# Left-over rows of a quadratic form: six passes from five operand tiles, and a 32-row by 64-column tiling for the rest

## The chip, the cores and the metric

The kernel runs on one core of one Trainium2 chip. The metric is the device time of one execution in microseconds (us); lower is better. The core has a matrix engine (TensorE, PE in the profile), a vector engine (VectorE, DVE), a scalar engine (ScalarE, ACT), GpSimd (POOL), and a queue engine for transfers (SyncE, SP). Each runs its own instruction stream; semaphores order them. SBUF is the on-chip memory of 128 partitions; PSUM, with eight banks of 512 float32 columns per partition, takes the results of TensorE.

## The reference

The input x has 1024 samples, 39 fields and 64 embedding columns. Three layers are computed; each is bilinear in the layer before and in x:

```python
def _cin_layer(Xk, X0, W, b):
    Wr = W.reshape(O, Hk, Fdim)
    return jnp.einsum('bhe,bfe,ohf->boe', Xk, X0, Wr) + b[None, :, None]
X0 = sparse_embedding; Xk = X0
for W, b in ((W0, b0), (W1, b1), (W2, b2)):
    Xk = _cin_layer(Xk, X0, W, b)
    outs.append(Xk.sum(axis=-1))
return jnp.concatenate(outs, axis=-1) @ fc_w.T + fc_b
```

All layers have 64 outputs. Only sums over the embedding columns, weighted by fc_w, leave the function, so the second and third layer can be folded. Call A the 64 outputs of the first layer before its bias: each is a weighted sum of the 780 products x_a x_b with a <= b. The rest of the answer is a sum over columns and over 64 rows of (A + b0) times Z, where each row of Z is again a weighted sum of the same 780 products, plus a weighted sum of the 39 fields themselves (the linear rows), plus a constant. Small terms from the biases b1 and b2 are added at the end.

## The kernel before, in words

**Blocks.** A column is one sample and one embedding index; there are 65,536. They are worked in 32 blocks of 2048 columns (`BLK`), two blocks to a pair, 16 pairs. One block fills four PSUM banks of 512 columns (`po[n][0..3]`); rows 0 to 63 of a bank hold A, rows 64 to 127 hold Z.

**Operand tiles.** The input is transposed by transfers to DRAM tables `xd` (field by column, with a row of ones after the 39 fields; three tables, each of two blocks). From a table, GpSimd gathers rows into operand tiles of 128 partitions by lists of row numbers (`gather_rows`, L124): four tiles of 128 x 2048 per block (`rt[n % 2][:, 0..3]`, filled by `roll`, L129), and two more per pair, `ut` and `vt`, whose 128 rows are 64 left-over rows of the first block and 64 of the second (`roll_half`, L134). The multiplication of two tiles by VectorE (`product`, L158) gives 128 rows of products; the lists are chosen so that the six pairs of the four tiles give 768 different products and linear rows, and the u-v product the 51 that are left of 819. `prods` has four buffers.

**Passes.** A chunk is one such product with its 128 x 128 weights `wa[:, c]` (64 columns for A, 64 for Z). `multiply` (L478) runs it over the four banks of the block. The chunk of left-over rows is run for both blocks: for each bank two matmuls of 64 rows and 128 columns, on rows 0 to 63 for block n and 64 to 127 for block n+1 (L485 to L493). Every float32 matmul appears in the trace as two matmul records and two weight loads.

**End of a block.** `finish` (L503): ScalarE reads Z of a bank with its constant into `z`, VectorE forms (A + b0) Z into `g`, and a reduction over the 64 embedding indices writes `sums`. `fields` (L495) copies the 39 fields of a block from `ut` into the lower rows of `g`, so that they are summed too.

**Order.** The program order is written out by hand (`manual_schedule`): `steps` lists the chunks, seven for an even block (the left-over chunk last) and six for an odd one. At each step (L583) PE gets the chunk, then possibly `finish` and `fields` of a block that closed a step ago, then VectorE the product four steps ahead (`AHEAD`), and after a block's last product GpSimd the gathers for the block two further on (L606 to L611). The inputs of later blocks are loaded by SP or GpSimd (`load`).

**Preparation.** L169 to L424 load and fold the weights into `both`; GpSimd and VectorE work out the row numbers (`lists`, L261 to L279 and L310 to L319); the first three operand tiles of block 0 are gathered in halves from `xh`, a first copy of the input. `weight_rows` (L427) forms 128 rows of weights of a chunk as runs along diagonals of `both` (one VectorE addition per run, or a ScalarE copy), and `weight_turn` (L463) transposes them on PE and copies them to `wa`. During the first pair this is interleaved with the steps.

Of the kernel before, what the change touches and what calls it, by code (L numbers as in the profile page):

```python
# [61 lines left out]
FH = F * H  # L62
NG = 3
K = NG * F
STEP = (0, 15, 9, 6)
BASE = (0, 3, 5, 20)
LAST = 11
EXTRA = (None, 6, 17, 28)
NX = 11
HR = 64  # L70
PAIRS = ((0, 1), (0, 2), (0, 3), (1, 2), (2, 3), (1, 3))
NPAIR = len(PAIRS)
ORDER = (0, 1, 3, 2, 4, 5)
NCHUNK = NPAIR + 1
# [9 lines left out]
FT = F + 1  # L84
NTAB = 3

_dist = sorted(
    min(d % F, -d % F)
    for i, k in PAIRS
    for j in range(NG)  # L90
    for d in [(STEP[k] - STEP[i]) * j + BASE[k] - BASE[i]]
)
assert sorted(_dist + [LAST]) == list(range(1, F // 2 + 1))
assert max(2 * s + b for s, b in zip(STEP, BASE)) < F
assert K + NX == 128 and EXTRA[1:] == tuple(6 + LAST * i for i in range(3))


@with_exitstack
def cin_kernel(ctx: ExitStack, tc: tile.TileContext, x, w0t, b0, w1, b1, w2, b2, fc_w, fc_b, out):
# [12 lines left out]
    xh = [dram.tile([FT, SUB], F32, name=f"xh{k}") for k in range(2)]  # L112
# [16 lines left out]
    def roll(n):  # L129
        for i in range(4):  # L130
            k = n % 2 * 4 + i
            gather_rows(rt[n % 2][:, i], xd[n // 2 % NTAB][: FT if k < 4 else 2 * FT], k)

    def roll_half(n):  # L134
        for k, dst in enumerate((ut, vt)):
            gather_rows(dst[n // 2 % 2], xd[n // 2 % NTAB], 8 + k)

    wa = const.tile([128, NCHUNK, 2 * H], F32, name="wa")
# [4 lines left out]
    b0s = const.tile([H, 1], F32, name="b0s")  # L143
# [5 lines left out]
    lists = const.tile([128, 10], I32, name="lists")  # L149
    rt = [const.tile([128, 4, BLK], F32, name=f"r{k}") for k in range(2)]  # L150
    ut = [const.tile([128, BLK], F32, name=f"u{k}") for k in range(2)]
    vt = [const.tile([128, BLK], F32, name=f"v{k}") for k in range(2)]
# [5 lines left out]
    def product(n, c, cols=slice(0, BLK), p=None):  # L158
        if p is None:
            p = prods.tile([128, BLK], F32, name="p", tag="p")  # L160
        if c < NPAIR:
            i, k = PAIRS[c]
            r = rt[n % 2]
            nc.vector.tensor_tensor(p[:, cols], r[:, i, cols], r[:, k, cols], ALU.mult)  # L164
        else:
            nc.vector.tensor_tensor(p, ut[n // 2 % 2], vt[n // 2 % 2], ALU.mult)  # L166
        return p

    prep = tc.tile_pool(name="prep", bufs=1)  # L169
    with prep as prep:  # L170
# [11 lines left out]
        shifts = prep.tile([128, 3, 3], F32, name="shifts")  # L182
# [13 lines left out]
        def load_half(k):  # L196
            nc.scalar.dma_start(
                xh[k][0:F].rearrange("f (b e) -> b f e", e=E), x[k * SB : (k + 1) * SB]
            )
# [12 lines left out]
        for i in range(3):  # L212
            for k, by in enumerate((STEP[i + 1], BASE[i + 1], EXTRA[i + 1] - K)):
                nc.gpsimd.memset(shifts[:, k, i : i + 1], float(by))
        for k in range(2):
            nc.gpsimd.dma_start(xh[k][F:FT].rearrange("r (p c) -> p r c", c=128), ones[0:8, 0:1])
# [26 lines left out]
        wide = prep.tile([128, 5, 3], F32, name="wide")  # L243
        fields_of = prep.tile([128, 6], F32, name="fields_of")
        third = prep.tile([128, 1], I32, name="third")
# [15 lines left out]
        row, f0, j, extra, t, half, q = new(), new(), new(), new(), new(), new(), new()  # L261
        field = [fields_of[:, i : i + 1] for i in range(6)]
        nc.vector.tensor_scalar(third, place, 171, None, ALU.mult)
        nc.vector.tensor_copy(row, place)
        nc.vector.tensor_scalar(parity[:, 1:2], place, 1, None, ALU.bitwise_and)
        nc.vector.tensor_scalar(third, third, 9, None, ALU.logical_shift_right)
        step(row, K, 1.0, extra)
        nc.vector.tensor_copy(f0, third)
        nc.vector.tensor_scalar(wide[:, 3], shifts[:, 2], row, None, ALU.add)
        fused(j, f0, -float(NG), row, ALU.mult, ALU.add)  # L270
        nc.vector.tensor_scalar(wide[:, 0], shifts[:, 1], f0, None, ALU.add)
        nc.vector.tensor_scalar(field[0], f0, float(F), None, ALU.min)
        fused(wide[:, 1], shifts[:, 0], j, wide[:, 0], ALU.mult, ALU.add)
        step(wide[:, 1], F, -float(F), wide[:, 2])
        nc.vector.tensor_tensor(wide[:, 1], wide[:, 1], wide[:, 2], ALU.add)
        nc.vector.tensor_tensor(wide[:, 4], wide[:, 3], wide[:, 1], ALU.subtract)
        fused(fields_of[:, 1:4], wide[:, 4], extra, wide[:, 1], ALU.mult, ALU.add)
        nc.vector.tensor_copy(lists[:, 0:4], fields_of[:, 0:4])
        nc.vector.tensor_scalar(lists[:, 4:8], fields_of[:, 0:4], float(FT), None, ALU.add)  # L279
# [5 lines left out]

        nc.gpsimd.memset(pairs, 0.0)
# [22 lines left out]

        step(row, HR, 1.0, half)  # L310
        fused(q, half, -float(HR), row, ALU.mult, ALU.add)
        nc.vector.tensor_tensor(field[4], q, step(q, F, -float(F)), ALU.add)
        nc.vector.tensor_tensor(field[4], field[4], step(q, 56, 11.0), ALU.add)
        nc.vector.tensor_scalar(field[5], q, float(F), None, ALU.min)
        fused(t, q, -50.0, step(q, 45, 1.0), ALU.add, ALU.mult)
        for y in (t, step(q, 50, -float(F)), step(q, 56, -6.0)):
            nc.vector.tensor_tensor(field[5], field[5], y, ALU.add)
        nc.vector.tensor_scalar(half, half, float(FT), None, ALU.mult)
        nc.vector.tensor_scalar(lists[:, 8:10], fields_of[:, 4:6], half, None, ALU.add)  # L319
# [7 lines left out]
        for k, cols in enumerate(halves):  # L327
            nc.sync.dma_start(xd[0][0:F, cols], xh[k][0:F])
        gather_rows(rt[0][:, 3], xd[0][:FT], 3)
# [38 lines left out]
        roll_half(0)  # L368
# [3 lines left out]
        nc.gpsimd.dma_start(b0s, b0.rearrange("(h o) -> h o", o=1))  # L372
# [54 lines left out]
    def weight_rows(c):  # L427
        def put(at, by, n, a, b, sa, sb, twice=True):
            out = pairs[:, c, at : at + by * (n - 1) + 1 : by]
# [5 lines left out]
            if twice:  # L435
                nc.vector.tensor_tensor(  # L436
                    out, diagonal(a, b, sa, sb), diagonal(b, a, sb, sa), ALU.add
                )
            else:
                nc.scalar.copy(out, diagonal(a, b, sa, sb))  # L440

        if c == NPAIR:
            put(0, 1, F, 0, 0, 1, 1, False)
            put(39, 1, 6, 0, F, 1, 0, False)
            put(45, 1, 5, 6, 34, 1, 1)
            put(50, 1, 6, 11, 0, 1, 1)
            put(56, 1, 6, 28, 0, 1, 1)
            nc.vector.tensor_copy(pairs[:, c, HR:], pairs[:, c, 0:HR])
            return
        i, k = PAIRS[c]  # L450
        if i == 0:
            put(K, 1, NX, EXTRA[k], F, 1, 0, False)
        elif k - i == 1:
            put(K, 1, NX, EXTRA[i], EXTRA[k], 1, 1)
        for j in range(NG):
            a, b = STEP[i] * j + BASE[i], STEP[k] * j + BASE[k]
            cuts = sorted({0, F - a, F - b, F})
            for lo, hi in zip(cuts, cuts[1:]):
                put(NG * lo + j, NG, hi - lo, (a + lo) % F, (b + lo) % F, 1, 1)

    turned = []

    def weight_turn(c):  # L463
# [6 lines left out]
        at = slice(place, place + 128)  # L470
        nc.tensor.transpose(tr[:, at], pairs[:, c], unit)  # L471
        nc.scalar.copy(wa[:, c], tr[:, at])  # L472
# [4 lines left out]

    def multiply(n, c, p, quarters=range(BLK // MM)):  # L478
        half = c == NPAIR
        for k in (n, n + 1) if half else (n,):  # L480
            if k not in po:
                po[k] = [bank("po") for _ in range(BLK // MM)]
        for m in quarters:

            for h in range(2 if half else 1):  # L485
                w = slice(h * HR, (h + 1) * HR) if half else slice(0, 128)
                nc.tensor.matmul(  # L487
                    po[n + h][m],
                    wa[w, c, :],
                    p[w, bass.ts(m, MM)],  # L490
                    start=c == opens[n + h],
                    stop=c == closes[n + h],
                )  # L493

    def fields(n):  # L495
        g[n] = []
        h = n % 2 * HR
        for m in range(BLK // SUB):
            gt = work.tile([H + F, SUB], F32, name="g", tag="g")
            nc.scalar.copy(gt[H : H + F], ut[n // 2 % 2][h : h + F, bass.ts(m, SUB)])  # L500
            g[n].append(gt)

    def finish(n):  # L503
        z = [work.tile([H, SUB], F32, name="z", tag="z") for _ in range(BLK // SUB)]
        for m in range(BLK // MM):
            nc.scalar.activation(  # L506
                z[m // 2][:, bass.ts(m % 2, MM)], po[n][m][H:128], AF.Identity, bias=fc0s[H:128]
            )
        for m in range(BLK // MM):
            at = bass.ts(m % 2, MM)  # L510
            gt = g[n][m // 2]
            nc.vector.scalar_tensor_tensor(  # L512
                gt[0:H, at], po[n][m][0:H], b0s, z[m // 2][:, at], ALU.add, ALU.mult
            )
            if m % 2:
                b_at = n * BB + m // 2 * SB
                nc.vector.tensor_reduce(  # L517
                    sums[:, b_at : b_at + SB], gt.rearrange("p (b e) -> p b e", e=E), AX.X, ALU.add
                )

    def finish_quarter(n, m):
        t = work.tile([H, MM], F32, name="zq", tag="zq")
        at = bass.ts(m % 2, MM)
        gt = g[n][m // 2][:, at]
        nc.scalar.activation(t, po[n][m][H:128], AF.Identity, bias=fc0s[H:128])  # L525
# [147 lines left out]
```

## Time and profile before

Three runs: 747.16, 748.48 and 750.84 us, median 748.48. One profiled execution:

| | |
|---|---|
| time of the profiled execution, first to last instruction (its span) | 749.0 us |
| first matmul on an operand tile (line 487) | at 20.6 us |
| last start of such a matmul | at 743.4 us |
| TensorE clock granted | 1.000 |
| matmul records of line 487 | 1792 (112 a pair) |
| one pair of blocks, middle of the run | 45.03 us |
| VectorE busy in such a pair | 39.2 us |
| GpSimd busy in such a pair | 19.1 us |
| DMA, mean over the span | 241 GB/s, 180.40 MB |
| gather of an operand tile, issue to landing | 5.0 / 7.8 / 13.2 us (least, median, most) |

The profile gives no other time for this execution than its span, so sums are made against 749.0 us. In a group of the profile, the number after x is the count of instructions; then the duration of one, or the busy time and the mean of one. "Idle before" is the time an engine stood still just before an instruction, and what ended it. PEld is the weight load of TensorE, which runs beside the matmuls. Matmul ends are modelled, so distances between starts are the better measure of TensorE's pace.

### The profile page before, as it was taken

Reading aid. Unit: us, or ns where it says so; the run is one execution under the profiler, and the core shown is the slowest. Engines: PE = TensorE matmul, PEld = TensorE weight load, DVE = VectorE, ACT = ScalarE, POOL = GpSimd, SP = SyncE. Lnnn points to the kernel's source line nnn. Section 1 sums busy time; section 2 is a strip of 40 time slices with the busy share of each in tenths; the row PEclk is TensorE's granted clock in tenths of the full one; section 3 lists DMA queues with packets and bytes.
Section 4 is the critical chain, followed back from the end, with each engine's and each line's share of the span. In section 5 each row is a group of like instructions: output and inputs, shape, how many; then the busy total and the mean of one; then the engine's idle time right before and its main releaser. Section 6 shows DMA issues by size and latency. Waiting matters only on the chain.

```text
span 749.0 us, 5258 instructions
## 1 busy us (share of the span) xinstructions
PE 744.8 (99%) x1895; PEld 328.9 (44%) x1895; DVE 644.6 (86%) x513; ACT 164.6 (22%) x226; POOL 320.2 (43%) x198
## 2 busy tenths in 40 slices
PE   9999999999999999999999999999999999999998
PEld 6444444444444444444444444444444444444443
DVE  5998898888889888898888889888899888898885
ACT  3132211221212222112221212222112221212222
POOL 7965633336243253633436243263532436343100
PEclk9999999999999999999999999999999999999999
DMA  9989675875757776575876757776565855747400
GB/s 303 380 280 410 212 287 183 336 258 200 292 163 277 258 288 246 183 280 193 336 240 212 280 178 281 259 275 249 182 287 197 336 224 187 271 141 300 168 1 0
DMA packets 58930, 180.40 MB, mean 241 GB/s; under 512 B 37172, under 2 KB 37237, under 8 KB 38808
## 3 DMA queue, kind: packets, MB, share of 16 engines
q0 software_dynamic: 24320, 169.44, 59.4%
q1 hardware_dynamic: 32894, 8.63, 5.0%
q10 hardware_dynamic: 1690, 1.99, 1.0%
q8 instruction: 15, 0.25, 0.1%
q14 instruction: 11, 0.09, 0.0%
HBM read 179.98 MB, written 10.60 MB: 254 GB/s over the span
## 4 chain that ended last, share of the span: by engine, by line
PE 99%; DVE 0%; ACT 0%; issue 0%
PE po L487 96%; PE idle L230 1%; PE pt L389 0%; PE pv L338 0%; PE pv L389 0%; PE pw L349 0%; PE pw L409 0%; PE tr L471 0%; PE pt L409 0%; PE small L296 0%; DVE g L526 0%; DVE sums L528 0%; ACT zq L525 0%; PE small L298 0%; DVE fc L301 0%
## 5 line engine op out<-in xcount | busy, mean ns | idle before, releaser
L487 PE MATMUL po<-p,wa 128*128 128x512 f32 (+1 forms) x1792 | 723.1, 595 | 0.0
L164 DVE TENSOR_TENSOR p<-r 128x2048 f32<-128x2048 f32 (+2 forms) x197 | 434.9, 2236 | 86.2 <-PE po L487 86.2
L487 PEld LDWEIGHTS po<-p,wa 128*128 128x128 f32 (+1 forms) x1792 | 314.0, 190 | 405.3 <-issue 383.7
L125 POOL DMA_INDIRECT r<-xd,lists x125 | 258.1, 2065 | 363.7 <-DVE p L164 336.6
L506 ACT ACTIVATE z<-po,fc0s 64x512 f32<-64x512 f32 x124 | 84.6, 683 | 356.5 <-PE po L487 349.7
L500 ACT COPY g<-u 39x1024 f32<-39x1024 f32 x64 | 66.7, 1043 | 180.2 <-DVE sums L517 180.1
L512 DVE SCALAR_TENSOR_TENSOR g<-po,b0s,z 64x512 f32<-64x512 f32 x124 | 86.4, 734 | 0.0
L517 DVE TENSOR_REDUCE sums<-g 103x16 f32<-103x1024 f32 x62 | 75.6, 1220 | 2.2
L166 DVE TENSOR_TENSOR p<-u,v 128x2048 f32<-128x2048 f32 x16 | 36.5, 2284 | 0.0
L125 POOL DMA_INDIRECT u<-xd,lists x16 | 28.3, 1772 | 4.9 <-issue 4.3
L125 POOL DMA_INDIRECT v<-xd,lists x16 | 15.3, 955 | 4.9 <-issue 4.9
L230 PE MATMUL idle<-const-float32-1.0 128*128 128x256 f32 (+1 forms) x16 | 7.3, 609 | 0.8 <-PEq L660 0.8
L526 DVE SCALAR_TENSOR_TENSOR g<-po,b0s,zq 64x512 f32<-64x512 f32 x4 | 3.0, 743 | 5.3 <-ACT zq L525 5.3
L125 POOL DMA_INDIRECT r<-xh,lists x6 | 5.8, 971 | 1.8 <-issue 1.5
L472 ACT COPY wa<-tr 128x128 f32<-128x128 f32 x7 | 1.9, 266 | 19.8 <-PE tr L471 19.8
L436 DVE TENSOR_TENSOR pairs<-both 128x6 f32<-128x6 f32 (+27 forms) x50 | 5.4, 178 | 0.5 <-ACT both L418 0.5
L230 PEld LDWEIGHTS idle<-const-float32-1.0 128*128 128x128 f32 x16 | 4.8, 328 | 1.6 <-issue 0.7
L119 POOL DMA_DIRECT2D xd<-in_x x5 | 5.2, 1063 | 0.0
L525 ACT ACTIVATE zq<-po,fc0s 64x512 f32<-64x512 f32 x4 | 2.7, 683 | 10.2 <-PE po L487 10.2
L528 DVE TENSOR_REDUCE sums<-g 103x8 f32<-103x512 f32 x4 | 2.7, 686 | 0.1
L624 PE MATMUL py<-sums,wfin 103*1 103x512 f32 (+2 forms) x6 | 2.1, 448 | 0.6 <-DVE sums L528 0.6
L389 PE MATMUL pt<-w1s,v 128*128 128x320 f32 x4 | 2.5, 779 | 0.0
(95 smaller groups left out, 54.0 us busy)
## 6 DMA issues: line engine op xcount, KB each, us to landing
xd<-in_x SPq DMA_DIRECT2D x26, 312.0 KB
r<-xd,lists POOLq DMA_INDIRECT x125, 7.8
xd<-in_x POOLq DMA_DIRECT2D x5, 312.0 KB, 6.1
w2s<-in_w ACTq DMA_DIRECT2D x1, 624.0 KB
w1s<-in_w ACTq DMA_DIRECT2D x2, 312.0 KB
xh<-in_x ACTq DMA_DIRECT2D x2, 156.0 KB
xd<-xh SPq DMA_DIRECT2D x2, 156.0 KB
u<-xd,lists POOLq DMA_INDIRECT x16, 8.9
```

What stands on the lines that cost most here:

```text
L119: engine.dma_start(xd[n // 2 % NTAB][first : first + F].rearrange("f (b e) -> f b e", e=E), xv[:, n * BB : (n + 1) * BB, :],)
L125: nc.gpsimd.indirect_dma_start(dst, None, table, bass.IndirectOffsetOnAxis(ap=lists[:, k : k + 1], axis=0))
L164: nc.vector.tensor_tensor(p[:, cols], r[:, i, cols], r[:, k, cols], ALU.mult)
L166: nc.vector.tensor_tensor(p, ut[n // 2 % 2], vt[n // 2 % 2], ALU.mult)
L230: nc.tensor.matmul(idle[:, 0:cols], nc.const_aps.tensor(1.0, (128, 128), F32), nc.const_aps.tensor(1.0, (128, cols), F32), start=True, sto ...
L436: nc.vector.tensor_tensor(out, diagonal(a, b, sa, sb), diagonal(b, a, sb, sa), ALU.add)
L487: nc.tensor.matmul(po[n + h][m], wa[w, c, :], p[w, bass.ts(m, MM)], start=c == opens[n + h], stop=c == closes[n + h],)
L500: nc.scalar.copy(gt[H : H + F], ut[n // 2 % 2][h : h + F, bass.ts(m, SUB)])
L506: nc.scalar.activation(z[m // 2][:, bass.ts(m % 2, MM)], po[n][m][H:128], AF.Identity, bias=fc0s[H:128])
L512: nc.vector.scalar_tensor_tensor(gt[0:H, at], po[n][m][0:H], b0s, z[m // 2][:, at], ALU.add, ALU.mult)
L517: nc.vector.tensor_reduce(sums[:, b_at : b_at + SB], gt.rearrange("p (b e) -> p b e", e=E), AX.X, ALU.add)
L526: nc.vector.scalar_tensor_tensor(gt[0:H], po[n][m][0:H], b0s, t, ALU.add, ALU.mult)
```

## The change

Five operand tiles take the place of four, and the six pairs are taken from them: (0,1), (0,2), (3,1), (3,2), (0,4), (3,4), in that order. The gathered rows are chosen anew. Six passes of 128 rows carry 768 of the 819 rows; of the 51 left, 30 are products and 21 linear rows. Both kinds get 32 rows per 1024 columns: `ut` and `vt` become 128 x 1024, and row group t (32 rows) holds columns t*1024 to t*1024 + 1023 of the pair of blocks. `join` runs them with matmuls of 32 rows and 64 columns: for each bank two on the product (A and Z), and one on `ut` itself for the linear rows, which only Z needs. So that these fall on different parts of the array, banks 1 and 3 of a block hold Z in rows 0 to 63 and A below (`wa` stores the A columns a second time behind Z; `finish_bank` reads accordingly). The left-over step now opens the banks of an odd block and closes those of an even one. `fields` copies from operand tile 0 in place of `ut`. In the preparation the fourth operand tile is gathered in halves from `xh` and the fifth from `xd`; the lists are worked out by other arithmetic.

```diff
-STEP = (0, 15, 9, 6)
-BASE = (0, 3, 5, 20)
-PAIRS = ((0, 1), (0, 2), (0, 3), (1, 2), (2, 3), (1, 3))
-ORDER = (0, 1, 3, 2, 4, 5)
-NCHUNK = NPAIR + 1
+NT = 5
+STEP = (0, 2, 2, 3, 1)
+BASE = (0, 35, 11, 1, 17)
+PAIRS = ((0, 1), (0, 2), (3, 1), (3, 2), (0, 4), (3, 4))
+SQUARE = 32
+NCHUNK = NPAIR + 2
...
-    def roll(n):
-        for i in range(4):
-            k = n % 2 * 4 + i
-            gather_rows(rt[n % 2][:, i], xd[n // 2 % NTAB][: FT if k < 4 else 2 * FT], k)
+    def roll(n, tiles=range(NT)):
+        for i in tiles:
+            k = n % 2 * NT + i
+            gather_rows(rt[n % 2][:, i], xd[n // 2 % NTAB][: FT if k < NT else 2 * FT], k)
-    def roll_half(n):
+    def roll_small(n):
+        table = xd[n // 2 % NTAB].rearrange("f (t c) -> (f t) c", c=SUB)
         for k, dst in enumerate((ut, vt)):
-            gather_rows(dst[n // 2 % 2], xd[n // 2 % NTAB], 8 + k)
+            gather_rows(dst[n // 2 % 2], table, 2 * NT + k)
...
-            nc.vector.tensor_tensor(p, ut[n // 2 % 2], vt[n // 2 % 2], ALU.mult)
+            nc.vector.tensor_tensor(p[:, 0:SUB], ut[n // 2 % 2], vt[n // 2 % 2], ALU.mult)
...
-        for k in range(2):
-            nc.gpsimd.dma_start(xh[k][F:FT].rearrange("r (p c) -> p r c", c=128), ones[0:8, 0:1])
...
+        for k, series in enumerate((U_STEPS, V_STEPS)):
+            for i, (at, by) in enumerate(series):
+                nc.gpsimd.memset(steps_at[:, k, i : i + 1], float(at))
+                nc.gpsimd.memset(steps_by[:, k, i : i + 1], float(by))
...
-        gather_rows(rt[0][:, 3], xd[0][:FT], 3)
+        for k, cols in enumerate(halves):
+            gather_rows(rt[0][:, 3, cols], xh[k], 3)
+        roll(0, (4,))
...
-        nc.scalar.copy(wa[:, c], tr[:, at])
+        nc.scalar.copy(wa[:, c, 0 : 2 * H], tr[:, place : place + 2 * H])
+        nc.scalar.copy(wa[:, c, 2 * H :], tr[:, place : place + H])
...
-            for h in range(2 if half else 1):
-                w = slice(h * HR, (h + 1) * HR) if half else slice(0, 128)
-                nc.tensor.matmul(
-                    po[n + h][m],
-                    wa[w, c, :],
-                    p[w, bass.ts(m, MM)],
-                    start=c == opens[n + h],
-                    stop=c == closes[n + h],
-                )
+            side = m % 2 * H
+            nc.tensor.matmul(
+                po[n][m],
+                wa[:, c, side : side + 2 * H],
+                p[:, bass.ts(m, MM)],
+                start=n % 2 == 0 and c == 0,
+                stop=n % 2 == 1 and c == NPAIR - 1,
+            )
+
+    def join(n, p):
+        open_block(n + 1)
+
+        def tiles(t, side):
+            rows = slice(SQUARE * t, SQUARE * t + SQUARE)
+            return rows, po[n + t // 2][2 * t % 4 + side]
+
+        for side in range(2):
+            for t in range(4):
+                for half in range(2):
+                    rows, dst = tiles(t, side)
+                    at = (side + half) * H
+                    nc.tensor.matmul(
+                        dst[half * H : half * H + H],
+                        wa[rows, NPAIR, at : at + H],
+                        p[rows, bass.ts(side, MM)],
+                        start=t >= 2,
+                        stop=t < 2 and half == side,
+                    )
+        for t in range(4):
+            for side in range(2):
+                rows, dst = tiles(t, side)
+                half = (1 - side) * H
+                nc.tensor.matmul(
+                    dst[half : half + H],
+                    wa[rows, NPAIR + 1, H : 2 * H],
+                    ut[n // 2 % 2][rows, bass.ts(side, MM)],
+                    start=False,
+                    stop=t < 2,
+                )
...
-            nc.scalar.copy(gt[H : H + F], ut[n // 2 % 2][h : h + F, bass.ts(m, SUB)])
+            nc.scalar.copy(gt[H : H + F], rt[n % 2][0:F, 0, bass.ts(m, SUB)])
...
+    def finish_bank(n, m, z):
+        one, other = slice(m % 2 * H, m % 2 * H + H), slice((m + 1) % 2 * H, (m + 1) % 2 * H + H)
+        nc.scalar.activation(z[one], po[n][m][other], AF.Identity, bias=fc0s[other])
+        at = bass.ts(m % 2, MM)
+        return lambda: nc.vector.scalar_tensor_tensor(
+            g[n][m // 2][0:H, at], po[n][m][one], b0s[one], z[one], ALU.add, ALU.mult
+        )
```

## The prediction

> **What bounds the kernel now.** I read the page first: busy shares, then the chain that ended last.
>
> ```profile
> PE 744.8 (99%) x1895; PEld 328.9 (44%) x1895; DVE 644.6 (86%) x513; ACT 164.6 (22%) x226; POOL 320.2 (43%) x198
> ...
> PE 99%; DVE 0%; ACT 0%; issue 0%
> PE po L487 96%; PE idle L230 1%; PE pt L389 0%; PE pv L338 0%; PE pv L389 0%; PE pw L349 0%; PE pw L409 0%; PE tr L471 0%; PE pt L409 0%; PE small L296 0%; DVE g L526 0%; DVE sums L528 0%; ACT zq L525 0%; PE small L298 0%; DVE fc L301 0%
> ```
>
> TensorE (PE) carries 99% of the chain, line 487 alone 96%. So time changes only where PE's stream changes, or where another engine begins to hold it up. Next the stream by stage: two successive pairs of blocks (columns: PE, PEld, DVE, ACT, POOL; clock; DMA share; GB/s).
>
> ```profile
> 314.20:359.23 45.03, 45.03 (x114) 19.62 (x113) 39.23 (x25) 9.64 (x12) 19.08 (x10) 1.00 0.67 247
> 359.23:404.26 45.03, 45.03 (x113) 19.62 (x113) 39.22 (x25) 9.64 (x12) 19.09 (x10) 1.00 0.69 245
> ```
>
> A pair lasts 45.03 us, PE never pauses, the clock is full. Inside the pair, the answer for line 487 in the stretch of the left-over rows:
>
> ```profile
> L487 PE MATMUL po<-p,wa x17: 589/589/693, 358.7 to 362.3; 64*128 64x512 f32 x16, 128*128 128x512 f32 x1
> ```
>
> Every float32 matmul is two records. A full one starts every 0.429 us (98 records in the 41.30 us from 362.90 to 404.20, edges included). The sixteen 64-row records start in couples 6 to 8 ns apart, one couple every 0.4225 us, from 359.229 to 362.344: the two row halves already work at once. From the last full start before them (358.706) to the second full start after (363.396) are 4.69 us; less two full slots (0.86), the stage costs 3.83 us: 8 slots x 0.4225 = 3.38, and 0.45 for going in and out (the four gaps at the edges are 0.523, 0.533, 0.519 and 0.533 in place of 0.42). Check: 96 x 0.429 + 3.83 = 45.02.
>
> So the change isn't from serial to parallel, it is from two tiles to eight. Is there anything here on tiles beside each other in columns? Yes, in the preparation:
>
> ```profile
> 6.84 2.40 PE L338 MATMUL pv<-w2s,fc 128*64 128x320 f32 x8
> ...
> 11.01 2.50 PE L389 MATMUL pt<-w1s,v 128*128 128x320 f32 x4
> ```
>
> Eight records of 64 columns take 2.40 us where four of 128 columns and the same 320-element stream take 2.50: two column tiles that read the same rows run at once, at no loss. And line 296 (one row, 64 columns[...]) shows a record of the upper column tile starting at 5.172 while three of the lower tile, earlier in the program, were still to start[...].
>
> [...]
>
> **The change part by part.**
>
> *Left-over rows.* Removed: 8 matmuls of 64 rows (16 records, 8 slots). Added: 16 product matmuls of 32 rows x 64 columns and 8 linear ones, 24 in all, 48 records. The loops give eight different tiles three times over (side 0, side 1, linear), so 3 x 2 = 6 slots of eight. 6 x 0.4225 = 2.535 against 3.38: 0.845 us less. Against it: a stagger of eight starts at 7 ns at the end of the pack (0.05 less the 0.007 of now), and increments. There are as many to post (four banks of n and the product's buffer), but all four banks now close in the last slot[...]. In and out stay 0.45. Net 0.79 us a pair, 16 pairs: **-12.6 us**. Bounds: 0.845 x 16 = -13.5; the other end is the first and second rival.
>
> *Full passes.* Six chunks of 128 rows x four quarters as before, 96 records a pair; the swapped halves in odd banks only move the start of the weight columns. 0.
>
> *Bank endings.* ScalarE and VectorE read the same 64x512 shapes (683 and 733 ns a piece), only from other partitions. 0. All four banks close at the end of the pack, so the first ScalarE read comes about 1.8 us later (362.1 in place of 360.3); VectorE reaches that ending only at 365.22, after a product, by when two ScalarE reads are done. Cover gone, it would cost VectorE 1 to 2 us a pair; it has 45.0 - 39.2 = 5.8 to spare.
>
> *Products.* 12 of 2.28 us as before; the last, 2.28 us over 2048 columns, becomes 1024 columns, 1.22 as the half products at the start take. VectorE: 39.2 - 1.1 = 38.1 in a pair of 44.2. A product starts when the buffer of four steps earlier is free and is done 2.3 us later; PE then has three steps (10.3 us) queued. Still hidden.
>
> *Gathers.* Two more 1 MB gathers a pair, and u and v at half size: +2.1 - 1.05 = +1.05 MB on 11.1 (247 GB/s x 45 us), so 12.2 MB in 44.2 us, 275 GB/s, share about 0.75 where slices of this profile reach 410 GB/s. GpSimd: +2 x 2.07 us on 19.1, 23 of 44. The first tile's gather waits in future for the fifth product of a block and for ScalarE's copy of the 39 fields out of it; copies end at 347.3, that product at about 348.3, where the gathers of the second tile on go out at 350.83 today. The five then need about 15 us of GpSimd and land 7.8 us (at most 13.2) after issue; the next product that reads the first two starts at 374.75, 24 us on. Behind them in GpSimd's queue stand u, v and the next block's gathers, which have a like margin. Hidden; without this cover each late microsecond would first eat the 8 us that products run ahead.
>
> *Preparation.* First matmul of line 487 at 20.62 us, behind the weights (second operand matrix landed at 6.8, then transposes and copies); none of that chain changes. GpSimd: two small DMAs of ones go (1.25 us), 26 more memsets 0.028 apart come (0.73): the first gather is some 0.4 us earlier. First list: 19 operations in place of 17 (+0.15 us), done by 3.6, needed at 6. One turn of weights more: +0.11 us on PE. Its ScalarE copy is split in two (+0.16 us a turn, the second part needed a matmul later). Weight rows on VectorE up to the fourth product: 28 additions (6, 6, 10, 6 in the timeline) become 35 (6, 8, 10, 11, counted from the new row lists), 0.09 us apart: +0.63 us, where that product was ready at 30.78 and PE takes it up at 32.7. The third step now reads the fourth tile, gathered seventh and eighth: issued about 15.4 and 16.6, plus 5.8 to land, 21.2 and 22.4; needed at 23.3 and 26.7. The fifth tile goes out at about 17.9 and, at 7.8 to 13.2 us, lands by 26 to 31; needed at 32. Sum: +0.1; bounds -0.4 to +4, the latter if that product or a gather is 2 to 4 us later than this.
>
> *Tail.* Same pieces: 0.
>
> Sum against the profiled execution: 749.0 - 12.6 + 0.1 = 736.5. That span is 0.5 above the median of the runs, 748.48, so **736.0 us** as a median, -1.7%.
>
> **Rivals.** *A short look-ahead (not all eight tiles fill).* At line 296 the other tile's record started only once no more than three were left ahead of it. If that limit holds over all tiles together, only four tiles start in the first slot, with their second records waiting; later slots mix four second records with four first ones: 7 slots. Gain 0.42 - 0.05 a pair, 6 us: 742.5. For it: that start. Against: three per tile explains it as well.
>
> *Slower: only row groups overlap.* Should the two column tiles of a 32-row group not run together, the 24 matmuls go four at a time: 12 slots x 0.4225 = 5.07 against 3.38, +1.69 x 16 = 27 us: 775.5. It decides from 8 slots on; nine would be 755.5. Against it: lines 338 and 296. For it: neither shows two column tiles beside four row groups, nor weight loads (224 ns for 64 columns) eight at a time.
>
> *A gain taken back by the feed.* A late tile in the first block or two stalls PE by 2 to 5 us, once, or the denser gathers in a burst (share 0.92 in that stretch already) hold up a product now and then: 739 to 741. For it: DMA is at 0.9 up to 75 us. Against: margins above.
>
> [...]
>
> **How the numbers follow.** 0.62 for the forecast (its own range 734.5 to 738), 0.15 for 742.5, 0.10 for slower (755 to 776), 0.09 for the feed, 0.04 for a mix near no change. About 0.5% is what a measurement of this kernel tells from no change: 744.7 to 752.2. Faster 0.62 + 0.15 + 0.09 less a little where these reach 744.7: 0.85; same 0.05; slower 0.10. The range leaves out the slower case and the mix (0.14): 733.5 to 744.
>
> **What would show it.** Left-over stage: records of 32 rows x 64 columns, 48 a pair, in six groups 0.42 us apart, 3.0 us in all in place of 3.83; pair 44.2 us; PE still 99%; VectorE 38.1 a pair; DMA about 275 GB/s. Seven groups mean the short look-ahead; twelve, the slower case; gaps of PE waiting for products after 20 us, the feed. I'm wrong if PE's share falls below 98%, or if the pair isn't shorter.

## The result, and the profile after

The changed kernel takes 742.43 us (median of 4 runs, 741.52 to 742.77), the kernel before 748.2 us (747.16 to 750.84): ratio 0.9919, 95% interval 0.9895 to 0.9942. It is faster, by less than half of what was forecast. The page, its busy shares and the chain that ended last:

```profile
span 740.5 us, 6425 instructions
...
PE 731.0 (99%) x2408; PEld 319.7 (43%) x2408; DVE 641.9 (87%) x521; ACT 167.1 (23%) x244; POOL 386.4 (52%) x256
...
PE 95%; DVE 3%; issue 1%; ACT 1%; DVEq 0%
PE po L535 88%; PE po L555 4%; PE po L566 2%; DVE p L211 1%; DVE pairs L503 1%; PE pt L454 0%; PE pv L402 0%; PE pv L454 0%; PE pw L413 0%; DVE wide L303 0%; PE idle L279 0%; ACT pairs L508 0%; ACT part L465 0%; PE small L351 0%; DVE g L585 0%
```

TensorE is still the bound, but the chain, 99% TensorE before, now has 3% of VectorE and 1% each of ScalarE and waiting: somewhere TensorE waits for a line of the two. `pairs L503` and `pairs L508` are lines that make weights, so it is in the first pair of blocks. First the middle of the run, two pairs by stage (columns as before: PE, PEld, DVE, ACT, POOL; clock; DMA share; GB/s):

```profile
314.45:358.61 44.16, 44.16 (x145) 19.11 (x145) 38.96 (x25) 9.63 (x12) 23.39 (x12) 1.00 0.75 282
358.61:402.77 44.16, 44.16 (x146) 19.11 (x145) 38.95 (x25) 9.63 (x12) 23.39 (x12) 1.00 0.74 276
```

and the left-over rows in TensorE's timeline (start, length, operation, count):

```profile
314.45 1.97 PE L555 MATMUL po<-p,wa 32*64 32x512 f32 x32
316.22 1.06 PE L566 MATMUL po<-u,wa 32*64 32x512 f32 x16
```

A pair went from 45.03 to 44.16 us. The single starts inside it come in six groups of eight, within 0.05 us each, at 358.61, 359.09, 359.52, 359.95, 360.38 and 360.81: all eight tiles work at once from the first group. Sixteen pairs at 0.874 us are 14.0 us. So where did the rest go? TensorE's timeline of the first pair:

```profile
32.69 0.27 PE L519 MATMUL tr<-unit,pairs 128*128 128x128 f32 x1
32.80 2.74 PE L535 MATMUL po<-p,wa 128*128 128x512 f32 x6
39.20 2.01 PE L535 MATMUL po<-p,wa 128*128 128x512 f32 x2 [3.66 <-ACT wa L520]
41.00 0.42 PE L519 MATMUL tr<-unit,pairs 128*128 128x128 f32 x1
41.21 4.35 PE L535 MATMUL po<-p,wa 128*128 128x512 f32 x8
```

At 32.69 the weights of the fifth chunk are turned; at 35.5 the fourth chunk is done; the fifth starts only at 39.20, after 3.66 us of idling for ScalarE's copy of those weights. Then two records take 2.01 us that take 1.0 at full speed. The clock that TensorE was granted (third figure from the end) shows why they are slow: in the 3.41 us from 39.30 on it was 0.50.

```profile
35.54:39.20 3.66, 0.00 (x0) 0.00 (x0) 3.66 (x10) 1.72 (x12) 3.66 (x4) 1.00 0.92 340
39.30:42.71 3.41, 3.41 (x5) 1.45 (x6) 1.38 (x1) 0.38 (x2) 3.09 (x5) 0.50 0.71 243
```

ScalarE's own timeline says where the wait comes from:

```profile
31.33 0.22 ACT L521 COPY wa<-tr 128x64 f32<-128x64 f32 x1
37.38 0.49 ACT L508 COPY pairs<-pairs 128x32 f32<-128x32 f32 x2 [5.83 <-DVE pairs L503]
37.78 0.68 ACT L501 COPY pairs<-both 128x10 f32<-128x10 f32 x6
38.49 0.49 ACT L508 COPY pairs<-pairs 128x32 f32<-128x32 f32 x2
38.89 0.26 ACT L520 COPY wa<-tr 128x128 f32<-128x128 f32 x1
```

The turned weights were ready at 33.0 and the copy takes 0.26 us, but it is issued behind four copies (line 508) that repeat the 32 left-over weight rows down the 128 partitions. These wait 5.83 us for VectorE, which forms the rows only after two products. The second of these and the seven additions of the rows:

```profile
34.53 2.28 DVE L211 TENSOR_TENSOR p<-r 128x2048 f32<-128x2048 f32 x1
36.73 0.61 DVE L503 TENSOR_TENSOR pairs<-both 128x9 f32<-128x9 f32 x7
```

The kernel before did the like copy on VectorE (its line 448), where it waits for nothing but the additions just before it.

The sum for the two profiled executions: first matmul on an operand tile at 20.17 in place of 20.62 (-0.45); from there to the first left-over stage 28.81 in place of 22.86 us (+5.95); sixteen pairs at -0.874 (-14.0). Together -8.5, as 749.0 and 740.5 show. The +5.95 have four parts:

- TensorE stands still: the fifth chunk's first record starts 4.25 us after the record before it, where 0.43 is usual (+3.83).
- Records at half the clock after it: starts 0.946, 0.853, 0.854 and 0.757 us apart in place of 0.43, and 0.214 in place of 0.11 after a turn (+1.80).
- The added turn of weights: 0.91 us from the turn before it to the next matmul on the operands, where a single turn takes 0.11. It waits 0.47 us for the second part of the copy of the turn before it (line 521) (+0.80).
- The kernel before ran more of its first records at half pace in its profiled execution (four take 2.43 us at 22.54, where they take 1.96 in the changed kernel) (-0.48).

The medians differ by 5.8, not 8.5. In the later runs a time is 1.7 to 1.9 us above its span, so the profiled execution of before, with a span of 749.0, is most likely the longest one listed, 750.84, while that of the changed kernel is an ordinary one.

### The profile page after: what moved, and what is told of

It reads as the page before. It is cut to its first block, busy times and chain, and to the rows that moved or that the text cites. A ratio compares the mean times of both kernels' runs of the same rounds, so it can differ in the third digit from the quotient of the medians.

```text
span 740.5 us, 6425 instructions
## 1 busy us (share of the span) xinstructions
PE 731.0 (99%) x2408; PEld 319.7 (43%) x2408; DVE 641.9 (87%) x521; ACT 167.1 (23%) x244; POOL 386.4 (52%) x256
## 4 chain that ended last, share of the span: by engine, by line
PE 95%; DVE 3%; issue 1%; ACT 1%; DVEq 0%
PE po L535 88%; PE po L555 4%; PE po L566 2%; DVE p L211 1%; DVE pairs L503 1%; PE pt L454 0%; PE pv L402 0%; PE pv L454 0%; PE pw L413 0%; DVE wide L303 0%; PE idle L279 0%; ACT pairs L508 0%; ACT part L465 0%; PE small L351 0%; DVE g L585 0%
## 5 line engine op out<-in xcount | busy, mean ns | idle before, releaser
L535 PE MATMUL po<-p,wa 128*128 128x512 f32 x1536 | 667.6, 595 | 3.7 <-ACT wa L520 3.7
L171 POOL DMA_INDIRECT r<-xd,lists x156 | 308.9, 1980 | 292.9 <-issue 281.5
L535 PEld LDWEIGHTS po<-p,wa 128*128 128x128 f32 x1536 | 290.9, 191 | 375.7 <-issue 352.0
L585 DVE SCALAR_TENSOR_TENSOR g<-po,b0s,z 64x512 f32<-64x512 f32 x128 | 95.9, 749 | 9.3 <-ACT z L583 5.3
L578 ACT COPY g<-r 39x1024 f32<-39x1024 f32 x64 | 66.7, 1043 | 152.1 <-DVE sums L596 124.6
L555 PE MATMUL po<-p,wa 32*64 32x512 f32 x512 | 31.6, 600 | 0.0
L171 POOL DMA_INDIRECT v<-xd,lists x16 | 28.5, 1782 | 4.9 <-issue 4.9
L213 DVE TENSOR_TENSOR p<-u,v 128x1024 f32<-128x1024 f32 x16 | 19.5, 1217 | 0.0
L555 PEld LDWEIGHTS po<-p,wa 32*64 32x64 f32 x512 | 9.4, 131 | 20.2 <-issue 20.2
L566 PE MATMUL po<-u,wa 32*64 32x512 f32 x256 | 17.0, 587 | 0.0
L503 DVE TENSOR_TENSOR pairs<-both 128x2 f32<-128x2 f32 (+27 forms) x59 | 6.1, 171 | 0.4 <-issue 0.3
L520 ACT COPY wa<-tr 128x128 f32<-128x128 f32 x8 | 2.1, 265 | 15.6 <-PE tr L519 15.6
```

The costliest lines, as they stand in the source:

```text
L171: nc.gpsimd.indirect_dma_start(dst, None, table, bass.IndirectOffsetOnAxis(ap=lists[:, k : k + 1], axis=0))
L213: nc.vector.tensor_tensor(p[:, 0:SUB], ut[n // 2 % 2], vt[n // 2 % 2], ALU.mult)
L503: nc.vector.tensor_tensor(out, diagonal(a, b, sa, sb), diagonal(b, a, sb, sa), ALU.add)
L535: nc.tensor.matmul(po[n][m], wa[:, c, side : side + 2 * H], p[:, bass.ts(m, MM)], start=n % 2 == 0 and c == 0, stop=n % 2 == 1 and c == NP ...
L555: nc.tensor.matmul(dst[half * H : half * H + H], wa[rows, NPAIR, at : at + H], p[rows, bass.ts(side, MM)], start=t >= 2, stop=t < 2 and ha ...
L566: nc.tensor.matmul(dst[half : half + H], wa[rows, NPAIR + 1, H : 2 * H], ut[n // 2 % 2][rows, bass.ts(side, MM)], start=False, stop=t < 2,)
```

## The experiments

Theory A: ScalarE's queue holds the fifth chunk's weights back. Theory B: the feed, a late product or gather. C and D are on the left-over stage.

**The four copies on VectorE.**

```diff
         if c >= NPAIR:
             for n in (SQUARE, 2 * SQUARE):
-                nc.scalar.copy(pairs[:, c, n : 2 * n], pairs[:, c, 0:n])
+                nc.vector.tensor_copy(pairs[:, c, n : 2 * n], pairs[:, c, 0:n])
```

> The changed kernel with the four copies that repeat the 32 left-over weight rows (line 508) on VectorE in place of ScalarE, nothing else. Theory A (ScalarE's queue): these copies wait on ScalarE for VectorE's rows (done at about 37.3 us), and the copy of the fifth chunk's weights stands behind them, so TensorE stands still from 35.5 to 39.2 us and then runs some records at half speed; without them in that queue the stall goes, about 3.7 us of wait and 1.7 us of half speed: 737.0 us (736 to 738), no gap over 1 us in the matmuls between 20 and 60 us. Theory B (the feed: a product or a gather comes late): nothing changes, 742.4 us, gap of 4.25 us stays.

Measured: 735.3 us (735.29 to 737.93), ratio to before 0.984 (0.9823 to 0.9858). TensorE's timeline from the turn of the fifth chunk's weights on:

```profile
33.96 0.27 PE L519 MATMUL tr<-unit,pairs 128*128 128x128 f32 x1
34.07 3.60 PE L535 MATMUL po<-p,wa 128*128 128x512 f32 x8
37.51 0.27 PE L519 MATMUL tr<-unit,pairs 128*128 128x128 f32 x1
37.62 3.60 PE L535 MATMUL po<-p,wa 128*128 128x512 f32 x8
41.05 0.27 PE L519 MATMUL tr<-unit,pairs 128*128 128x128 f32 x1
41.80 0.33 PE L519 MATMUL tr<-unit,pairs 128*128 128x128 f32 x1 [0.47 <-ACT wa L521]
```

No gap is left but the 0.47 us at the added turn. From the first matmul to the first left-over stage this execution takes 23.61 us in place of 28.81, 5.2 less where 5.4 were expected. Theory B has no room: the edit leaves gathers and products as they were. The median fell by 7.1, 1.9 more than the 5.2; that part lies ahead of the first matmul (see the end of the next section).

**The same copies on ScalarE, later in its order.** `fill_rows` holds the same four scalar copies, taken out of `weight_rows`.

```diff
             weight_turn(steps[at + 1][1])
+            if at == NPAIR - 2:
+                fill_rows(NPAIR)
+                fill_rows(NPAIR + 1)
```

> The changed kernel with the same four copies on ScalarE, only issued later in its order: behind the copy of the sixth chunk's weights instead of ahead of the fifth's. Theory A: the order alone is what costs, so the gain is that of the move to VectorE, 737.0 us (736 to 738). If the load on ScalarE or VectorE were what costs, or theory B holds: 742.4 us.

Measured: 736.65 us (735.35 to 737.9), ratio 0.985 (0.9834 to 0.9867). The fourth and fifth chunk in TensorE's timeline:

```profile
31.73 3.60 PE L536 MATMUL po<-p,wa 128*128 128x512 f32 x8
35.17 0.27 PE L520 MATMUL tr<-unit,pairs 128*128 128x128 f32 x1
35.28 3.60 PE L536 MATMUL po<-p,wa 128*128 128x512 f32 x8
```

Same engine, same instructions, another place in the queue: the gain is the same within the spread, and the stretch up to the first left-over stage takes 23.67 us, beside 23.61. It is the order that costs, not the load on ScalarE.

**The other way round: the kernel before with its copy on ScalarE.**

```diff
-            nc.vector.tensor_copy(pairs[:, c, HR:], pairs[:, c, 0:HR])
+            nc.scalar.copy(pairs[:, c, HR:], pairs[:, c, 0:HR])
```

> The kernel before with its one copy that repeats left-over weight rows (line 448) moved from VectorE to ScalarE, nothing else. Theory A: the same queue forms, ScalarE waits for VectorE's rows until about 37.2 us with the fifth chunk's weights behind it, TensorE stands still 3 to 4 us and restarts at half speed: 4 to 6 us slower than before, about 753. Theory B: no difference, within 1 us of before.

Measured: 750.46 us (748.92 to 751.52), ratio 1.0033 (1.002 to 1.0047). ScalarE's and TensorE's timelines:

```profile
33.93 0.24 ACT L448 COPY pairs<-pairs 128x64 f32<-128x64 f32 x1 [5.67 <-DVE pairs L436]
34.08 0.26 ACT L472 COPY wa<-tr 128x128 f32<-128x128 f32 x1
```

```profile
29.37 2.74 PE L487 MATMUL po<-p,wa 128*128 128x512 f32 x6
34.40 1.13 PE L487 MATMUL po<-p,wa 128*128 128x512 f32 x2 [2.29 <-ACT wa L472]
```

The same queue appears in the other kernel. The cost, 2.3 us, is below the 4 to 6 expected: one copy stands in the way and not four with six more between them (34.08 - 33.93 = 0.15 us in place of 38.89 - 37.38 = 1.5 us), and after 2.88 us from one start to the next (0.43 is usual) the records behind it were not slowed as in the changed kernel: two took 1.13 us, not 2.01, and the next eight 3.60, not 4.35.

**TensorE kept busy while it waits.**

```diff
+        if at == 4:
+            busy = bank("busy")
+            for _ in range(4):
+                nc.tensor.matmul(
+                    busy,
+                    nc.const_aps.tensor(1.0, (128, 128), F32),
+                    nc.const_aps.tensor(1.0, (128, MM), F32),
+                    start=True,
+                    stop=True,
+                )
```

> The changed kernel with four matmuls of ones (128x512, eight records, 3.4 us) put on TensorE ahead of the fifth chunk's first matmul, where it stands still; their results are not used. The wait for the weights stays. Theory A in two parts: the wait (3.7 us) is the same, the half speed after it (about 1.7 us) goes, 740.7 us; if the slow records after the stall have another cause, 742.4 us or, if the filling delays the fifth chunk, above.

Measured: 739.94 us (739.71 to 740.69), ratio 0.9898 (0.9884 to 0.9913).

```profile
34.12 3.61 PE L669 MATMUL busy<-const-float32-1.0 128*128 128x512 f32 x8
38.40 1.13 PE L535 MATMUL po<-p,wa 128*128 128x512 f32 x2 [0.67 <-ACT wa L520]
39.37 0.27 PE L519 MATMUL tr<-unit,pairs 128*128 128x128 f32 x1
39.48 3.60 PE L535 MATMUL po<-p,wa 128*128 128x512 f32 x8
```

The wait for the weights stayed, the slow records went: eight take 3.60 us at once, not 4.35, and two 1.13, not 2.01. From the fifth chunk's first record to the left-over stage it is 8.09 us in place of 9.78: 1.7, as expected. The median fell by 2.5; in the two traces the fifth chunk also starts 0.8 us earlier, because the first matmul on an operand tile starts 1.24 us earlier while the way from there to the fifth chunk is 0.44 longer. In the changed kernel, then, the stall's price has two parts: 3.83 us of standing still, and 1.80 on the records behind it.

**Z in the same rows of all banks.** This takes back one named part of the change, on top of the first experiment's kernel (735.3 us).

```diff
-            side = m % 2 * H
+            side = 0
...
-                    at = (side + half) * H
+                    at = half * H
...
-                half = (1 - side) * H
+                half = H
...
-        one, other = slice(m % 2 * H, m % 2 * H + H), slice((m + 1) % 2 * H, (m + 1) % 2 * H + H)
+        one, other = slice(0, H), slice(H, 2 * H)
...
```

The lines left out give `z` the shape that it had in the kernel before.

> On top of the kernel with the copies on VectorE (735.3 us): Z stays in rows 64 to 127 of all four banks, so the eight linear matmuls fall on the four upper column tiles, two on each, instead of one on each of eight. Theory C (a slot holds one record per tile, whatever the tile): product part 4 slots as before, linear part 4 slots instead of 2, stage 8 slots; +0.858 us a pair, 16 pairs, 749.0 us (747.5 to 750.5), VectorE and ScalarE as before. Theory D (the group of eight is not what sets the stage, for instance the weight loads or the first slot do): less than 5 us slower.

Measured: 750.08 us (749.55 to 752.34), ratio to before 1.002 (1.0009 to 1.0031). The stage in TensorE's timeline:

```profile
312.85 1.97 PE L555 MATMUL po<-p,wa 32*64 32x512 f32 x32
314.62 1.96 PE L566 MATMUL po<-u,wa 32*64 32x512 f32 x16
```

The product part is unchanged, the linear part takes 1.96 in place of 1.06 us, as long as the four groups of the product part (1.97). A pair lasts 45.05 us (312.85 to 357.90). Theory C's figure, 749.0 us, is met within 1.1. A stage of eight slots of 0.43 us is what the kernel before had, with a pair of 45.03 us, so here the smaller tiles by themselves gained nothing; the swap in the odd banks, which spreads the linear rows over all eight tiles, brought the two slots.

**The same 24 matmuls, tile by tile.** Each tile's linear matmul follows its two product matmuls.

```diff
-        for side in range(2):
-            for t in range(4):
-                for half in range(2):
+        for t in range(4):
+            for half in range(2):
+                for side in range(2):
...
+                side = 1 - half
...
```

> On top of the kernel with the copies on VectorE (735.3 us): the same 24 matmuls of the left-over rows, issued tile by tile (all three of one tile, then the next tile). Look-ahead of three records per tile, as read from line 296: a tile's first record waits until the tile before has only three of its six left, two slots later each time, so 14 + 6 = 20 slots in place of 6, +6.0 us a pair, 831 us. Look-ahead deep enough for all 48 records: 735.3 us. A look-ahead shared by all tiles: between these or above, above 780 us.

Measured: 847.17 us (846.95 to 849.01), ratio 1.1315 (1.1281 to 1.1349). Part of one stage:

```profile
299.63 1.07 PE L555 MATMUL po<-p,wa 32*64 32x512 f32 x4
300.49 0.59 PE L564 MATMUL po<-u,wa 32*64 32x512 f32 x1
300.54 0.64 PE L555 MATMUL po<-p,wa 32*64 32x512 f32 x2
300.91 0.59 PE L564 MATMUL po<-u,wa 32*64 32x512 f32 x1
300.97 0.64 PE L555 MATMUL po<-p,wa 32*64 32x512 f32 x2
...
306.46 0.59 PE L555 MATMUL po<-p,wa 32*64 32x512 f32 x1
306.89 1.02 PE L564 MATMUL po<-u,wa 32*64 32x512 f32 x2
307.84 41.47 PE L535 MATMUL po<-p,wa 128*128 128x512 f32 x96
349.23 1.07 PE L555 MATMUL po<-p,wa 32*64 32x512 f32 x2
```

From 300.49 to 305.49 the starts come in twelve groups of three; two groups of two stand ahead of them (the four records from 299.63 on), and 2, 2, 1, 1 behind. A stage opens with two groups of one (the two records from 349.23 on). That makes 20 groups of 1, 1, 2, 2, twelve times 3, 2, 2, 1, 1, the sizes that eight tiles of six records give if each begins two groups after the tile before it, as assumed for 831 us. 847 were measured, since groups are 0.43 to 0.49 us apart and not 0.43, and the granted clock is 0.982. The time alone would also fit a look-ahead shared by all tiles, put above 780 us; but with three waiting records for all tiles together the kernel's own order would start only four tiles in its first group, and it starts eight. So of the two, only a count for each tile agrees with both orders. The number three in it is an estimate of mine, from one start at line 296 and these group sizes; what lets a record start was not shown.

## Why the prediction was right or wrong

*The bound and the left-over stage: right.* Six groups, 99% TensorE, a pair of 44.2 us forecast and 44.16 measured. The gain of 0.79 us a pair was 0.874, 1.3 us more over the run. One reading was off: couples of 64-row records are 0.429 us apart (359.762 to 362.337, six steps), as full records are, and not 0.4225. So the stage of before is 8 x 0.429 and 0.40 for going in and out, where the prediction had 0.45. In the changed kernel going in and out costs 44.16 - 96 x 0.4292 - 6 x 0.429 = 0.38 us, with the stagger (eight starts within 0.05 us) and the increments in it: nothing that had been set against the two slots shows. (Of the 0.79 us forecast, 0.80 less 0.01, the 0.01 for increments was an estimate of mine that no trace had shown.)

*Full passes, products, gathers, bank endings: hidden, as said.* DMA moves 276 to 282 GB/s at a share of 0.75 (275 and 0.75 forecast), GpSimd is busy 23.4 us a pair (23), and VectorE's products wait only for TensorE. VectorE is busy 38.96 us a pair where 38.1 was forecast; with Z in the same rows it is 38.33, so most of the excess belongs to the reading of odd banks. I had taken that for 0; it stays hidden.

*The preparation: wrong.* This is the step that failed: "One turn of weights more ... Sum: +0.1; bounds -0.4 to +4". It cost 5.5 us on balance (-0.45 + 5.95). VectorE's added rows (+0.63 us) were harmless: the fourth product was ready at 30.78, the very time of before. What was left out is the last lines of `weight_rows`: the copies of the repeated rows change from VectorE to ScalarE. Nothing was asked of them: what they wait for, and what is queued behind them. That queue cost 3.83 us of standing still and 1.80 of half clock. Two experiments from one side (copies moved, copies issued later) and one from the other (the kernel before with its copy on ScalarE) show that this wait is the cost. The upper bound failed too, because the records at half the clock (0.50 for 3.41 us) were not in it. A smaller term was off as well: the added turn, put at 0.11 us, cost 0.80, since the second part of the split copy, said to be needed a matmul later, is waited for by the next turn.

*The rivals.* The short look-ahead forecast 742.5 us, and 742.4 is what was measured: a coincidence. The trace has eight starts in the first group, not four. The order of the records does count: tile by tile, at most three start in a group. "A gain taken back by the feed" had the right shape, one stall of 2 to 5 us in the first blocks, and the wrong cause: no gather and no product was late. The slower rival, column tiles that don't run together, is refuted by the same groups of eight.

*The size.* Without the queue the same change measures 735.3 us, beside the 736.0 of the forecast. That it comes so close is in part luck. The forecast took the span of 749.0 as 0.5 above the median; a time is some 1.8 above its span, so 749.0 belongs to an execution that started late. From that execution to the profiled one with the copies on VectorE, which starts as late, it is 749.0 to 736.1, with 736.5 forecast: -14.0 in the pairs (-12.6 forecast), +0.75 up to the first left-over stage and +0.4 ahead of it (+0.1 forecast for both).

*Where runs of one kernel differ.* The profiled executions cut at four points (us; the fourth turn is that of the fourth chunk's weights):

| execution | first matmul on an operand tile | from there to the fourth turn | to the first left-over stage | to the end |
|---|---|---|---|---|
| before | at 20.62 | 11.16 | 11.70 | 705.47 |
| before, copy on ScalarE | at 16.84 | 10.59 | 14.25 | 705.46 |
| changed | at 20.17 | 10.69 | 18.12 | 691.51 |
| changed, copies on VectorE | at 21.02 | 11.11 | 12.50 | 691.51 |
| changed, copies later | at 18.63 | 11.17 | 12.50 | 691.51 |
| changed, TensorE kept busy | at 18.93 | 10.68 | 16.88 | 691.50 |

For one kernel the last column is the same to 0.01 us, and the one before it holds the price of the queue. What varies beside it is the start and, by up to 0.6 us, the first steps. The preparation also ran at another pace in one execution than in another: the ten transposes of `part` into `pw`, begun at 15.6 us in both, took 1.28 us in the kernel before and 0.82 in the changed one, whose first matmul starts 0.45 us earlier. In the changed kernel the granted clock is on record from 15.4 us on: 1.00 up to 18.8, 0.50 up to 22.2, then 1.00 up to 39.3. (The granted clock of 1.000 listed for the kernel before covers only what is on record, from 23.6 us on.) The starts of the changed kernel's variants lie 2.4 us apart, as the runs of one of them do (735.29 to 737.93). A difference in the start also accounts for the 1.9 us of the first experiment if its faster runs, with spans of 733.5, started at about 18.4 (an estimate: 733.5 less the rest of its trace). *Open:* what sets the start of an execution, and whether it is chance that none of the four runs of the changed kernel started as early.

## What to carry to other kernels

When a copy moves to another engine, look at that engine's queue and not at its load: what does the instruction wait for, and who needs the one behind it? Four copies of 0.2 us each, on an engine that is 77% idle, cost 5.6 us because they stood in front of weights. With small matmuls, look at the order of the tiles: here 24 of them took six groups of starts with two records to each tile before coming round, and twenty tile by tile (735.3 and 847.2 us). And look for a rest that sits on half of the tiles: with the linear rows on four of eight the gain was gone (750.1 us).

## What the runs showed of the hardware that was not expected

The same 24 matmuls took six groups of eight starts in the kernel's own order, and twenty groups of at most three tile by tile: 735.3 against 847.2 us for the kernel.

In the changed kernel, after 3.66 us without matmuls, the granted clock was 0.50 for 3.41 us (two records in 2.01 us for 1.0). In the kernel before with its copy on ScalarE, after 2.29 us without them, two records took 1.13 us and the next eight 3.60; in the changed kernel with other matmuls in the wait, of which 0.67 us were left, the same 1.13 and 3.60. In the tile-by-tile run TensorE is busy in all of the 100 us from 300 on, and yet the mean granted clock in them was 0.98:

```profile
300.00:400.00 100.00, 100.00 (x283) 43.53 (x280) 76.64 (x50) 19.27 (x24) 41.57 (x23) 0.98 0.63 235
```

Why it was below 1 there is open.

And in the changed kernel VectorE's pieces for the odd banks, which read rows 64 to 127 and write rows 0 to 63, took 754 to 757 ns, those for the even banks 742 to 744, and the second of two began 0.77 us after the first. In the kernel before, with Z in the same rows of all banks, they took 731 to 743 and began 0.66 us apart.
